# Perceiver block on one core: reductions over the partitions moved from TensorE to VectorE's 32x32 transposes

## The chip, the cores and the metric

The kernel runs on one core of a Trainium2 chip. The metric is device time in microseconds, the median of several runs. The profile is one execution taken by the hardware profiler; its span runs from the first to the last instruction of the core. PE is TensorE's matmuls, PEld its weight loads, DVE is VectorE, ACT is ScalarE, POOL is GpSimd, SP is SyncE.

## What is computed

For each of 16 batches, with x of 128 x 512 and a context of 2048 x 512, all in float32:

```python
x = x + softmax(layernorm(x) @ ctx.T) @ ctx            # cross-attention, one head
x = x + self_attention(layernorm(x))                   # 16 heads of 32, rotary half, causal, then @ Wc
h = layernorm(x)
logits = h[0] @ Wr.T                                   # router: the first token alone, 8 experts
top_vals, top_idx = top_k(logits, 2)                   # gates: softmax over the two
x = x + h + sum(gate[e] * (h @ A[e].T) @ Bw[e].T for e in top_idx)
```

In the last line the expert layer adds its own input h, so that `res` in the kernel starts as x2 + h.

## The kernel before

The work is a software pipeline over the batches. Python generators (`score`, `attend`, `inner`, `experts`) each issue a batch's work in pieces, and the main loop (`for b in range(B - 2)`) steps them by hand so that four batches are under way at once. The order on TensorE is the order of the program, since every matmul, transpose by TensorE and DMA on the SP and ACT queues is kept in program order (`matmul`, `transpose`, `load`). On VectorE, ScalarE and GpSimd a scheduler may move instructions, save those that are `pinned` to the program's order. Helper lines carry most records: line 115 issues for VectorE, ScalarE and GpSimd, line 137 every matmul, 140 every transpose by TensorE, 145 every DMA; so groups are told apart by the tiles' names.

- `score(b)` (from line 376) makes the transposed scores of the cross-attention: the 2048 context rows lie on the partitions (in four blocks of 512, each as four rows per partition), the 128 queries along the free dimension. Matmuls write `psc`, ScalarE copies them to `sc`, VectorE takes the running maximum `mx`. The maximum and the sum of a query's softmax therefore have to be taken over the partitions. For the maximum, `mx` is folded to 128 x 128, TensorE transposes it (`tr_m`), VectorE reduces (`nm`), writes `nm` on a diagonal (`diag`), and a matmul of ones by `diag` (`spread`) brings it to all partitions. VectorE adds `spread` to `sc`, and ScalarE takes the exponentials. `sums` adds up the exponentials of the four blocks, and is folded to `part` (128 x 128).
- `attend(b)` (from line 453) multiplies `sc` with the context in four quarters (`av`); a matmul of `part` by a column of ones gives each query's sum (`den`), its reciprocal is `rden`, and `x1` is `av` times `rden` plus x. The layernorm of x1 follows (`st`, `mv`, `rs`, `h`; `rs`, the root, is GpSimd's).
- `inner(b)` (from line 504) is the self-attention: `v`, `k`, `q` projections, the rotary part (VectorE's shuffle `kP` and product `kT`, GpSimd's product on `kP`, VectorE's add to `kT`; the same for q), head masks `kb` on ScalarE, scores `pss`, softmax in four groups of heads (`att`, `nmx`, `rsm`), transposes of it (`pX`, by way of DRAM to `pT`), `y`, the output product `o`, and `x2`.
- `experts(b)` (from line 889) takes the layernorm of x2 (transposed by way of DRAM to `hT3`). The router multiplies the first token's column with `w_r` (`g_share`) and adds up 4 chunks (`g_part`, 128 x 8); a matmul of ones by `g_part` (`lg`) sums over the partitions and leaves the logits on every partition. `choose` takes the two largest, GpSimd gathers their weights by indirect DMA (`each`, `wb`; `wa` is a copy in another layout), and matmuls `mid` and `ffn` follow; `res` is the result, which a DMA on GpSimd's queue writes out.

In one pass of the main loop TensorE's order is: y of batch b - 1, v of b, tr_m of b + 1, o of b - 1, spread of b + 1, k and q of b, the first quarter of av of b + 1, pss of b, the other quarters of av, den of b + 1, lg of b - 1, psc of b + 2 with mid and ffn of b - 1 inside it. The last batches follow an order written out by hand (`CLOSING`).

A fold and the moves by TensorE, which the change touches:

```python
def halved(t, op):
    vector.tensor_tensor(t[:, :2], t[:, :2], t[:, 2:], op)
    vector.tensor_tensor(t[:, 0], t[:, 0], t[:, 1], op)
    return t[:, 0]
...
transpose(tr[:, :S], most, ident)
vector.tensor_reduce(nm, tr[:, :S], AX.X, ALU.max, negate=True)
vector.tensor_scalar(diag, ident, nm, None, ALU.mult)
matmul(spread[:, :S], ones, diag, start=True, stop=True)
```

Of the kernel before, what the change touches and what calls it, by code (L numbers as in the profile page):

```python
# [11 lines left out]
F32 = mybir.dt.float32  # L12
I32 = mybir.dt.int32
U32 = mybir.dt.uint32
# [75 lines left out]
def perceiver_block(ctx: ExitStack, tc: tile.TileContext, io: dict, out: bass.AP):  # L90
# [40 lines left out]

    padded = const.tile([P, KC, QD], F32, name="padded")
    gpsimd.memset(padded, 0.0)


    def matmul(*args, **kwargs):
# [47 lines left out]
    def norm_pieces(src, name, n=P, tag="h", mix=False):  # L184
        stats = Later(p2, [P, 6], tag="stats", name=f"st_{name}")
        mv = Later(p2, [P, 2], tag="mv", name=f"mv_{name}")
        rstd = Later(p2, [P, 1], tag="rstd", name=f"rs_{name}")
        h = Later(p2 if tag == "h" else p1, [P, D], tag=tag, name=f"{tag}_{name}")

        def root():  # L190
            eps = gpsimd.tensor_scalar_add(rstd[:n], mv[:n, 1:2], EPS)
            if name == "1_1":
                pinned(eps)
            gpsimd.tensor_tensor(rstd[:n], rstd[:n], mhalf[:n], ALU.pow)

        def norm():
            to, of = (mixed(h[:n]), plain(src[:n])) if mix else (h[:n], src[:n])
            return vector.tensor_scalar(to, of, mv[:n, 0:1], rstd[:n], ALU.subtract, ALU.mult)

        return h, [  # L200
            lambda: vector.bn_stats(stats[:n], src[:n]),
            lambda: vector.bn_aggr(mv[:n], stats[:n]),
            root,
            norm,
        ]
# [68 lines left out]
    def named(b, **of):  # L274
        for name, piece in of.items():
            pieces[f"{name}.{b}"] = piece
# [78 lines left out]
    def first_norm(x, hT):  # L355
# [8 lines left out]
        for c in range(KC):  # L364
# [7 lines left out]
            scalar.copy(hT[:, :, c, :], tr[:, :P].rearrange("p (a j) -> p a j", a=4))  # L372
            warm_up(1)


    def score(b):

        hT = p1.tile([P, 4, KC, QD], F32, tag="hT1" if b != 1 else "hT3", name=f"hT1_{b}")
        if b:
            h = layernorm(xs[b], f"1_{b}", mix=b == 1)  # L380
            yield
            transposed(h[:], hT, f"1_{b}", b == 1)
        else:
            first_norm(xs[b], hT)
            yield
        yield

        sc = p2.tile([P, VC, 4, S], F32, tag="sc", name=f"sc_{b}")
        mx = p1.tile([P, 4, S], F32, tag="mx", name=f"mx_{b}")
        for v, ct in enumerate(turned_cts.pop(b)):  # L390
            ps = bank(ps_sc, "sc", f"psc_{b}_{v}").rearrange("p (j t) -> p j t", j=4)
            for j in range(4):

                if v == VC - 1 and j == 3:
                    yield
                for c in range(KC):
                    matmul(
                        ps[:, j, :].rearrange("p (a i) -> p a i", a=4),
                        ct[:, c, j * P : (j + 1) * P], hT[:, :, c, :],
                        start=(c == 0), stop=(c == KC - 1),  # L400
                    )
            scalar.copy(sc[:, v], ps)

            if v:
                vector.tensor_tensor(mx, ps, mx if v > 1 else sc[:, 0], ALU.max)
            if v < VC - 1:
                yield
# [4 lines that stand above are left out]
            return t[:, 0]  # L412

        most = halved(mx, ALU.max)
        yield

        tr = bank(ps_tr, "tr", f"tr_m_{b}")
        transpose(tr[:, :S], most, ident)
        nm = p2.tile([P, 1], F32, tag="nm", name=f"nm_{b}")
        vector.tensor_reduce(nm, tr[:, :S], AX.X, ALU.max, negate=True)  # L420
        diag = p1.tile([P, S], F32, tag="diag", name=f"diag_{b}")
        vector.tensor_scalar(diag, ident, nm, None, ALU.mult)
        yield
        spread = bank(ps_tr, "tr", f"spread_{b}")
        matmul(spread[:, :S], ones, diag, start=True, stop=True)
        for v in range(VC):
            vector.tensor_tensor(
                sc[:, v], sc[:, v], spread[:, None, :S].to_broadcast([P, 4, S]), ALU.add
            )
            scalar.activation(sc[:, v], sc[:, v], AF.Exp)  # L430
        part = p2.tile([P, S], F32, tag="part", name=f"part_{b}")
        scores[b] = (sc, part)
        yield
        sums = p1.tile([P, 4, S], F32, tag="sums", name=f"sums_{b}")
        pinned(vector.tensor_tensor(sums, sc[:, 0], sc[:, 1], ALU.add))
        yield
        for v in range(2, VC):
            pinned(vector.tensor_tensor(sums, sums, sc[:, v], ALU.add))

        def fold():  # L440
            vector.tensor_tensor(sums[:, :2], sums[:, :2], sums[:, 2:], ALU.add)

        def last_fold():
            vector.tensor_tensor(part, sums[:, 0], sums[:, 1], ALU.add)

        if b == B - 1:
            named(b, fold=fold, last_fold=last_fold)
        else:
            fold()
            last_fold()  # L450
        yield

    def attend(b):

        sc, part = scores.pop(b)
        acc = bank(ps_acc, "acc", f"av_{b}")
        ct = cts.pop(b)

        def quarter(v):
            for j in range(4):  # L460
                matmul(
                    acc, sc[:, v, j, :], ct[v][:, j, :],
                    start=(v == 0 and j == 0), stop=(v == VC - 1 and j == 3),
                )

        state = {}

        def whole():
            den = state["den"] = bank(ps_tr, "tr", f"den_{b}")
            matmul(den[:, :1], part, ones[:, :1], start=True, stop=True)  # L470

        rden = Later(p2, [P, 1], tag="rden", name=f"rden_{b}")

        def inverse():
            vector.reciprocal(rden[:], state["den"][:, :1])

        x1 = Later(p2, [P, D], tag="x1", name=f"x1_{b}")

        def added():
            vector.scalar_tensor_tensor(x1[:], acc, rden[:], xs.pop(b), ALU.mult, ALU.add)  # L480

        if b == B - 1:
            quarter(0)
            named(
                b, av1=lambda: quarter(1), av2=lambda: quarter(2), av3=lambda: quarter(3),
                den=whole, rden=inverse, x1=added,
            )
            h, norm = norm_pieces(x1, f"2_{b}", mix=True)
            named(b, **dict(zip(("st2", "mv2", "rs2", "h2"), norm)))
            firsts[b] = x1, h  # L490
            yield
            return
        for v in range(VC):
            quarter(v)
            if v == (VC - 1 if b else VC - 2):
                whole()
                inverse()
            if v < VC - 1:
                yield
        added()  # L500
        firsts[b] = (x1, layernorm(x1, f"2_{b}", mix=b == 0))
        yield

    def inner(b):
# [254 lines left out]
    def shares(b, first):  # L759

        share, part = small(b, E * KC, "share"), small(b, E, "part")
        share = share.rearrange("p (e c) -> p e c", e=E)
        mult = vector.tensor_tensor(
            share,
            w["r"].rearrange("p c e -> p e c"),
            first[:, None, :].to_broadcast([P, E, KC]),
            ALU.mult,
        )
        pinned(mult)
        vector.tensor_reduce(part[:], share, AX.X, ALU.add)  # L770
        return part

    def routing(b):


        z, top, best = small(b, E, "z"), small(b, 8, "top"), small(b, 8, "best", U32)
        at, row, rows = small(b, TOP, "at"), small(b, 1, "row"), small(b, 1, "rows", I32)
        blocks = small(b, TOP, "blocks", I32)

# [7 lines left out]

        def logits(part):

            banks.append(bank(ps_tr, "tr", f"lg_{b}"))  # L790
            matmul(banks[0][:, :E], ones, part[:], start=True, stop=True)

        def choose():
            vector.tensor_copy(z[:], banks[0][:, :E])
            vector.max(top[:], z[:])

            vector.max_index(best[:], top[:], z[:])
            vector.tensor_copy(at[:], best[:, :TOP])
            vector.tensor_scalar(blocks[:], at[:], float(P), column(C_P), ALU.mult, ALU.add)
            vector.tensor_scalar(row[:], at[:, 1:2], column(C_TWOR), column(C_RANK), ALU.mult, ALU.add)  # L800
# [7 lines left out]
                ))  # L808

        def gather_second():  # L810
            gpsimd.indirect_dma_start(
                wb[:], None, io["BT"], bass.IndirectOffsetOnAxis(ap=rows[:], axis=0)
            )

        def joined():

# [72 lines left out]
    def experts(b):  # L889
# [9 lines left out]
        if b < B - 1:  # L899
# [5 lines left out]

            if b < B - 3:
                share()
                yield
                logits(state["part"])
                for piece in rest[:4]:  # L910
                    piece()
                yield
# [137 lines left out]
    for b in range(B - 2):  # L1050
# [17 lines left out]
        step(inner, b)  # L1068
        step(attend, b + 1)
        step(experts, b - 1)  # L1070
        step(inner, b)
        step(experts, b - 1)
        step(inner, b + 1)
# [85 lines left out]
```

## Time and profile before

| what | value |
|---|---|
| time, median of 3 runs | 810.46 us (810.45 to 811.42) |
| the profiled execution's own time | 810.97 us |
| its span | 809.2 us |
| mean granted TensorE clock | 0.998 |
| ACT, POOL busy | 260.4 us, 146.6 us |
| moved by DMA | 211.05 MB, mean 261 GB/s |

In the profile's rows, a start and a duration in us come first, then the engine, the helper's line, the operation, the tile written and those read, shapes and a count; in brackets stands how long the engine had been idle, and what ended it. Equal neighbours are merged into one row. Matmuls overlap: a matmul's duration is its way through the array, so its price in a full queue is the distance from its start to the next one's start. A float32 matmul is two records.

### The profile page before, as it was taken

The page shows a single profiled execution, that of the slowest core. Times are in us where ns is not written, and L with a number is a line of the kernel's source. Part 1 is how long each engine was busy: PE and PEld are TensorE (multiplying, and loading weights), DVE is VectorE, ACT ScalarE, POOL GpSimd, SP SyncE. Part 2 cuts the span into 40 slices and gives each one's busy share as a digit, 9 for nine tenths or more (in the row PEclk, how much of TensorE's full clock was granted, in tenths as well). Part 3 has the DMA queues.
Part 4 walks back from the last instruction along what each step waited for, and adds up shares of the span by engine and source line. Part 5 has one row for each costly group of instructions (what it writes and reads, how often), then busy time and mean ns, then how long its engine had stood idle before and what let it go on. Part 6 is the DMA issues. An engine that isn't in the chain of part 4 may idle for free.

```text
span 809.2 us, 14363 instructions
## 1 busy us (share of the span) xinstructions
PE 800.2 (99%) x5538; PEld 568.5 (70%) x5538; DVE 529.7 (65%) x1234; ACT 260.4 (32%) x772; POOL 146.6 (18%) x213
## 2 busy tenths in 40 slices
PE   9999999999999999999999999999999999999996
PEld 9946775768677576866758677676867757686653
DVE  2455759386684947658495775938667584856885
ACT  2232324142232423233241232415223241422461
POOL 1001011212121121211112121111212112121204
PEclk9999999999999999999999999999999999999999
DMA  9998394967849497694958859495885949664102
GB/s 375 417 389 321 118 380 171 340 253 251 360 163 381 172 324 292 221 397 142 364 212 292 320 188 399 152 353 222 281 337 181 388 152 340 261 231 173 41 1 79
DMA packets 76868, 211.05 MB, mean 261 GB/s; under 512 B 6400, under 2 KB 42624, under 8 KB 60416
## 3 DMA queue, kind: packets, MB, share of 16 engines
q10 hardware_dynamic: 15696, 113.32, 35.0%
q1 hardware_dynamic: 57168, 84.75, 29.4%
q0 software_dynamic: 3936, 12.07, 4.4%
q8 instruction: 44, 0.72, 0.3%
q14 instruction: 24, 0.20, 0.1%
HBM read 180.23 MB, written 29.88 MB: 260 GB/s over the span
## 4 chain that ended last, share of the span: by engine, by line
PE 97%; DVE 1%; POOL 0%; issue 0%; ACT 0%; POOLq 0%
PE psc L137 28%; PE av L137 28%; PE k L137 7%; PE q L137 7%; PE v L137 7%; PE o L137 6%; PE pss_sc L137 2%; PE y L137 2%; PE ffn L137 2%; PE pss_acc L137 2%; PE mid L137 2%; PE warm L137 1%; PE tr_m L140 0%; PE tr L140 0%; PE spread L137 0%; PE lg L137 0%
## 5 line engine op out<-in xcount | busy, mean ns | idle before, releaser
L137 PE MATMUL psc<-hT,ctxT 128*128 128x128 f32 x2048 | 235.0, 276 | 0.0
L137 PEld LDWEIGHTS psc<-hT,ctxT 128*128 128x128 f32 x2048 | 231.3, 192 | 0.5 <-issue 0.5
L137 PE MATMUL av<-ctx,sc 128*128 128x512 f32 x512 | 227.3, 596 | 0.0
L137 PEld LDWEIGHTS av<-ctx,sc 128*128 128x128 f32 x512 | 94.4, 190 | 110.5 <-issue 107.9
L115 ACT ACTIVATE att<-att,nmx 128x128 f32<-128x128 f32 x256 | 98.8, 388 | 84.9 <-DVE nmx L115 84.9
L115 POOL TENSOR_SCALAR rs<-mv 128x1 f32<-128x1 f32 x47 | 10.6, 225 | 431.0 <-DVE g_at L115 209.5
L115 ACT COPY sc<-psc 128x512 f32<-128x512 f32 x64 | 37.5, 586 | 140.0 <-PE psc L137 140.0
L115 ACT ACTIVATE sc<-sc 128x512 f32<-128x512 f32 x64 | 40.2, 630 | 90.9 <-DVE sc L115 90.4
L137 PE MATMUL k<-hT,w_k 128*128 128x128 f32 x512 | 60.1, 275 | 0.0
L137 PE MATMUL q<-hT,w_q 128*128 128x128 f32 x512 | 60.0, 275 | 0.0
L137 PEld LDWEIGHTS k<-hT,w_k 128*128 128x128 f32 x512 | 58.5, 192 | 1.5 <-issue 0.8
L137 PE MATMUL v<-w_v,hT 128*32 128x512 f32 x520 | 59.0, 593 | 0.0
L137 PEld LDWEIGHTS q<-hT,w_q 128*128 128x128 f32 x512 | 58.5, 192 | 0.0
L137 PE MATMUL o<-w_c,yT 128*128 128x512 f32 x128 | 57.8, 594 | 0.0
L115 DVE TENSOR_TENSOR mx<-psc,mx 128x512 f32<-128x512 f32 x32 | 21.6, 676 | 55.0 <-ACT sc L115 55.0
L115 ACT ACTIVATE kb<-kT,cst 128x512 f32<-128x512 f32 (+1 forms) x34 | 36.2, 1113 | 39.8 <-DVE kT L115 39.8
L115 DVE TENSOR_SCALAR h<-x,mv,rs 128x512 f32<-128x512 f32 x47 | 27.4, 583 | 31.9 <-POOL rs L115 31.9
L115 ACT ACTIVATION_READ_ACCUMULATOR att<-att,nmx 128x1 f32 x256 | 47.9, 187 | 0.0
L115 DVE TENSOR_TENSOR sc<-sc,spread 128x512 f32<-128x512 f32 x64 | 42.6, 671 | 3.3 <-PE spread L137 3.3
L115 DVE TENSOR_TENSOR att<-att,rsm 128x512 f32<-128x512 f32 x64 | 43.4, 678 | 0.8
L115 DVE TENSOR_REDUCE nmx<-att 128x4 f32<-128x512 f32 x64 | 41.8, 671 | 0.1
L137 PEld LDWEIGHTS o<-w_c,yT 128*128 128x128 f32 x128 | 23.9, 196 | 23.8 <-issue 23.0
(139 smaller groups left out, 851.1 us busy)
## 6 DMA issues: line engine op xcount, KB each, us to landing
ctx<-in_ctx_dram ACTq DMA_DIRECT2D x56, 1024.0 KB, 8.4
ctxT<-in_ctxT_dram ACTq DMA_DIRECT2D x52, 1024.0 KB, 10.5
there_p<-pX SPq DMA_DIRECT2D x28, 512.0 KB, 4.0
pT<-there_p SPq DMA_DIRECT2D x28, 512.0 KB, 4.5
ctxT<-in_ctxT_dram SPq DMA_DIRECT2D x12, 1024.0 KB, 8.9
there<-blocks SPq DMA_DIRECT2D x42, 256.0 KB, 3.3
hT<-there SPq DMA_DIRECT2D x42, 256.0 KB, 3.0
ctx<-in_ctx_dram SPq DMA_DIRECT2D x8, 1024.0 KB, 10.5
```

What stands on the lines that cost most here:

```text
L115: ins = issue(*args, **kwargs)
L137: tc.keep_in_program_order(nc.tensor.matmul(*args, **kwargs))
```

## The change

For batches from 2 on, the maximum over the partitions no longer goes through TensorE; for batches 2 to 14 the sum doesn't either, and for batches 0 to 12 the router's sum doesn't. A new function does it on VectorE: 32x32 transposes within the tile, a reduction along the free dimension, which leaves one value per quadrant (32 partitions), copies of three quadrants' values to the first quadrant, a second reduction, and then transposes of a broadcast (or four copies of a column) which bring the result to the partitions of all quadrants. More instructions are pinned, the exponentials are issued in two parts, the sums of a batch are pinned behind them and so ahead of the next self-attention's rotary part, `attend` has one step more, and the router's sum follows `share` at once.

```diff
+    beside = const.tile([P, QD], F32, name="beside")
+    gpsimd.memset(beside, 0.0)
...
+    def across(t, name, op, negate=False):
+        n = t.shape[1] // QD
+        turned = p1.tile([P, n, QD], F32, tag="diag" if n == 4 else "turned_1", name=f"turned_{name}")
+        pinned(vector.transpose(turned.rearrange("p q i -> p (q i)"), t))
+        each = p2.tile([P, 4, n], F32, tag=f"each_{n}", name=f"each_quadrant_{name}")
+        pinned(vector.tensor_reduce(each[:, 0, :], turned, AX.X, op))
+        for a in range(1, 4):
+            pinned(vector.tensor_copy(each[:QD, a, :], each[a * QD : (a + 1) * QD, 0, :]))
+        whole = p2.tile([P, n], F32, tag=f"whole_{n}", name=f"whole_{name}")
+        pinned(vector.tensor_reduce(
+            whole[:QD], each[:QD].rearrange("p a q -> p q a"), AX.X, op, negate=negate
+        ))
+        return whole[:QD]
...
+        if b > 1:
+            spread = p1.tile([P, 4, QD], F32, tag="spread", name=f"spread_{b}")
+            peak = across(most, f"m_{b}", ALU.max, negate=True)
+            for a in range(4):
+                pinned(vector.transpose(
+                    spread[a * QD : (a + 1) * QD], peak[:, :, None].to_broadcast([QD, 4, QD])
+                ))
+            for v in range(VC):
+                pinned(vector.tensor_tensor(
+                    sc[:, v], sc[:, v],
+                    spread.rearrange("p j i -> p (j i)")[:, None, :].to_broadcast([P, 4, S]), ALU.add,
+                ))
+                if v < 2:
+                    scalar.activation(sc[:, v], sc[:, v], AF.Exp)
+            yield
+            for v in range(2, VC):
+                pinned(scalar.activation(sc[:, v], sc[:, v], AF.Exp))
...
+            pinned(vector.tensor_tensor(sums, sc[:, 0], sc[:, 1], ALU.add))
+            yield
+            for v in range(2, VC):
+                pinned(vector.tensor_tensor(sums, sums, sc[:, v], ALU.add))
+            yield
+            whole = across(halved(sums, ALU.add), f"den_{b}", ALU.add)
+            vector.reciprocal(whole, whole)
+            rden = p2.tile([P, 1], F32, tag="rden", name=f"rden_{b}")
+            for a in range(4):
+                vector.tensor_copy(rden[a * QD : (a + 1) * QD], whole[:, a : a + 1])
+            scores[b] = (sc, rden)
...
-            if v == (VC - 1 if b else VC - 2):
+            if not known and v == (VC - 1 if b else VC - 2):
                 whole()
                 inverse()
...
-        firsts[b] = (x1, layernorm(x1, f"2_{b}", mix=b == 0))
+        h, norm = norm_pieces(x1, f"2_{b}", mix=b == 0)
+        for piece in norm[:3]:
+            piece()
+        if b:
+            yield
+        pinned(norm[3]())
+        firsts[b] = x1, h
...
+            if b < B - 3:
+                whole = across(part, f"lg_{b}", ALU.add)
+                for a in range(4):
+                    pinned(vector.transpose(
+                        z[a * QD : (a + 1) * QD], whole.to_broadcast([QD, QD])
+                    ))
+                return
...
                 share()
+                logits(state["part"])
                 yield
-                logits(state["part"])
...
         step(experts, b - 1)
+        step(attend, b + 1)
         step(inner, b)
```

On VectorE's queue this puts, in one pass, the whole maximum and the four adds to `sc` and the first add of `sums` ahead of `x2`; the transpose of the third layernorm (`blocks`) and the other two adds of `sums` between `x2` and the shuffle `kP`; the first fold of `sums` (128 x 256) between the product and the add of `kT`, the second (128 x 128) behind that add; the transpose of the sums between the product and the add of `qT`; the rest of the sum between `qT` and the first mask of the self-attention's softmax; and the router's sum between the last groups of that softmax and `x1`. On ScalarE two of the four exponentials stand ahead of the copy `vv` and of the four loads of `ctxT` that follow it. TensorE's order is the same but for the matmuls that are gone.

## Prediction

> **What bounds the kernel now.** I read the page first: the busy row and the chain that ended last.
>
> ```profile
> PE 800.2 (99%) x5538; PEld 568.5 (70%) x5538; DVE 529.7 (65%) x1234; ACT 260.4 (32%) x772; POOL 146.6 (18%) x213
> ...
> PE 97%; DVE 1%; POOL 0%; issue 0%; ACT 0%; POOLq 0%
> ```
>
> PE is in use 99% of the span and carries 97% of the chain. A busy PE need not be at its peak, so next I read one pass of the main loop in the timeline, PE alone.
>
> ```profile
> 393.28 1.08 PE L137 MATMUL y<-pT,vv 128*32 128x128 f32 x32
> ...
> 397.72 0.33 PE L140 MATMUL tr_m<-ident,mx 128*128 128x128 f32 x1
> 397.89 3.60 PE L137 MATMUL o<-w_c,yT 128*128 128x512 f32 x8
> 401.32 0.39 PE L137 MATMUL spread<-diag,ones 128*128 128x128 f32 x2
> 401.55 3.74 PE L137 MATMUL k<-hT,w_k 128*128 128x128 f32 x32
> ...
> 408.69 3.60 PE L137 MATMUL av<-ctx,sc 128*128 128x512 f32 x8
> 412.22 1.13 PE L137 MATMUL pss_sc<-kb,qT 64*128 64x256 f32 x8
> ...
> 424.55 0.28 PE L137 MATMUL den<-ones,part 128*128 128x1 f32 x2
> 424.69 0.37 PE L137 MATMUL lg<-g_part,ones 128*128 128x8 f32 x2
> 424.92 0.91 PE L137 MATMUL psc<-hT,ctxT 128*128 128x128 f32 x6
> ...
> 441.14 1.08 PE L137 MATMUL y<-pT,vv 128*32 128x128 f32 x32
> ```
>
> From y to y is 47.86 us, the same in thirteen passes from 106 us on: PE never waits for data here, so a matmul taken out is worth its own start-to-start time, as long as nothing else comes late. What comes latest shows in VectorE's and GpSimd's timeline ahead of pss, which needs qT.
>
> ```profile
> 401.53 0.69 DVE L115 TENSOR_TENSOR x<-o,x 128x512 f32<-128x512 f32 x1 [2.82 <-PE o L137]
> ...
> 405.10 0.55 DVE L115 TENSOR_SCALAR h<-x,mv,rs 128x512 f32<-128x512 f32 x1 [0.43 <-POOL rs L115]
> ...
> 406.17 0.73 DVE L115 STREAM_SHUFFLE kP<-k 128x512 f32<-128x512 f32 x1
> 406.98 1.28 POOL L115 TENSOR_TENSOR kP<-kP,cst 128x512 f32<-128x512 f32 x1 [1.91 <-DVE kP L115]
> 408.29 0.69 DVE L115 TENSOR_TENSOR kT<-kT,kP 128x512 f32<-128x512 f32 x1 [0.20 <-POOL kP L115]
> 409.12 0.74 DVE L115 STREAM_SHUFFLE qP<-q 128x512 f32<-128x512 f32 x1
> 411.31 0.69 DVE L115 TENSOR_TENSOR qT<-qT,qP 128x512 f32<-128x512 f32 x1 [0.89 <-POOL qP L115]
> ```
>
> qT is ready at 411.31 + 0.69 = 412.00 and pss starts at 412.22. In the tail, where PE does wait, tr follows the end of h by 0.05 us (800.03 to 800.08). So only 0.22 - 0.05 = 0.17 us of cover is left at pss. That is the place of this prediction.
>
> **What the change takes off PE.** Start to start, unrounded: tr_m 0.166, spread 0.221, den 0.140, lg 0.223, together 0.750 us a pass. Passes 1 to 13 lose all four; the score of b = 15 loses the first two (0.39). If PE never waited: 13 x 0.750 + 0.39 = 10.1 us. The built order on PE is otherwise unchanged.
>
> **What it adds to VectorE.** Each reduction is a 32x32 transpose, a reduce, three copies between quadrants, a reduce, and four more moves or transposes. Rows near: 128-wide operations take 0.29 us, tiny ones 0.14 to 0.18. Maximum: 0.29 + 0.29 + 3 x 0.14 + 0.17 + 4 x 0.29 = 2.3, less nm and diag (0.58): +1.7. Sum: 0.29 + 0.29 + 0.42 + 0.17 + 0.16 + 4 x 0.14 = 1.9, less rden: +1.75. Router: about 1.6, less the copy g_z: +1.5. So some 5 us a pass beside 32.5 us of VectorE work in 47.86: VectorE doesn't become the bound. What counts is where they stand.
>
> *Maximum, up to x2.* From the start of y: the last mx at -0.14 (441.00 against 441.14); with 0.73, 0.46 and 0.33 the transpose is at 1.37, the reduce at 1.71, res at 1.92 (ends 2.60), copies from 2.63. No row shows a move between quadrants. The Trainium skill (VectorE: DVE Perf Modes, Two Vector instructions with no wait between them) says that an instruction whose start quadrant changes is held until all earlier ones have finished. Unheld, small rows follow each other by 0.05 to 0.1 us and 128-wide ones by 0.21 (g_nm to mv 0.05, mx to res 0.21); held, by their length and 0.035: 0.175 and 0.33. Unheld the three copies and four transposes take about 1.1 us, held 1.9. I take held: second reduce 3.16, transposes from 3.36, the four adds of sc from 4.70 at 0.605 each, sums at 7.11, VectorE free at 7.72. x2 can start at 401.53 - 393.28 = 8.25, less tr_m's 0.17: 8.08. Cover 0.36 us held, about 1.1 unheld; either way x2 isn't late. Below nothing it can't go, since x2 waits for o.
>
> *From x2 to qT.* x2 follows o, but k now starts right behind o: against PE's program x2 comes 0.22 later. Before, sc's adds filled the waits of the layernorm chain x2, st, mv, rs, h. Now they are done before, and what used to stand behind qT (two adds of sums) and the transpose of h stand between h and kP. By rows: x2 to st 0.73, st to mv 0.73, mv to h 1.18, h to blocks 0.58, blocks to the next 0.64, sums to sums 0.80, to kP 0.60: 5.26 us, where it was 406.17 - 401.53 = 4.64. That is +0.62.
>
> Between the kT multiply and kT's add now stands the fold of sums (128x256, two inputs in SBUF), while GpSimd multiplies kP. No row has just this pair; the nearest is in the tail:
>
> ```profile
> 793.90 0.95 POOL L115 DMA_INDIRECT wb<-in_BT_dram,g_rows  x1 [0.30 <-issue]
> ...
> 794.45 1.08 DVE L115 TENSOR_TENSOR res<-x,h 128x512 f32<-128x512 f32 x1
> ...
> 751.27 0.68 DVE L115 TENSOR_TENSOR res<-x,h 128x512 f32<-128x512 f32 x1
> ```
>
> The same add takes 0.68 alone and 1.08 beside GpSimd: it ends 0.68 after GpSimd's end (794.85 to 795.53), so it waited it out. The skill (SBUF — State Buffer, Who interferes with whom) says the same of a VectorE instruction with two SBUF inputs beside a GpSimd one that reads SBUF: the later is blocked whole. POOL's kP starts 0.08 after the shuffle and takes 1.28; the fold comes 0.4 into it, is blocked to its end, takes 0.42, and kT's add follows 0.34 after POOL's end where it was 0.03: +0.31. Without the block the fold is free. I take the block (row and rule agree), and keep 0 as the other bound. The second fold and den's transpose stand in waits that last longer.
>
> qT is then late by 0.22 + 0.62 + 0.31 - 0.17 = 0.98 us, and PE waits that long ahead of pss, with av, psc and all else in its queue behind. kb is at hand 0.5 us ahead of that (0.78 ahead of pss before).
>
> *Hidden.* The rest of the sum stands between qT and the first mask, which it holds to about y + 21.0 (before: 414.90 - 393.28 = 21.62). The router's steps put x1 some 1.2 us later; behind it h2's way through SP's queue ends 4.8 us ahead of v (hT issued 434.20, 3.0 to land, v 442.03) and wa 3.2 us ahead of mid (435.17, 438.40): covered. On ACT two exps now stand ahead of vv, so vv's copy and the four ctxT loads behind it come 2.2 to 2.7 us later; q needs vv's bank 4 us after that, ctxT is used at y + 31.6 and lands by about y + 20. The pinned GpSimd gathers keep their place; the memset is once.
>
> **Sum.** A pass: -0.750 + 0.98 = +0.23. Thirteen: +3.0. The score of b = 15: no adds of sums and no fold ahead of kP, its shuffle at x2 + 3.9, no wait: -0.39. Together +2.6. The profiled execution took 810.97 with a span of 809.2; it is 0.5 above the median, so 813.6 for it is 810.46 + 2.6 = 813.1 for the median.
>
> **Rivals.**
> - *Likeliest, 42%*: as above, 813.1 (812.0 to 814.5 for 0.1 us either way at pss).
> - *No block, 17%*: the fold runs beside POOL's kP. Wait 0.67, a pass -0.08, together -1.5: 808.9. For it: the row that shows a block has an indirect DMA on POOL, not a multiply.
> - *Copies blocked too, 25%*: POOL issues out's DMA (0.67 us) 0.3 after res, at y + 2.9 to 3.56, just where the third copy between quadrants stands. If it waits that out, the adds of sc end 0.58 later, x2 is 0.22 late, a pass +0.45: about 816. Against it: no row shows such a DMA blocking a tiny copy.
> - *Faster, 8%*: the wait at pss doesn't arise, since kP's shuffle comes within 4.64 - 0.22 + 0.17 = 4.6 us of x2. From there PE keeps all it is given: 810.46 - 10.1 = 800.3. For it: DVE has 15 us free a pass. Against: seven rows make the 5.26, and the instructions' order is fixed. Each 0.1 us between is worth 1.3 us.
> - *Slower still, 8%*: moves between quadrants or transposes of 32 partitions cost over 0.1 us more than the nearest rows, beyond the 0.36 of cover, or the waits lower PE's clock (0.5 in the tail behind waits of 2.6 and 0.7 us): over 817.5. Against the clock: the tail's first wait of 0.7 us left it at 1.
>
> The range leaves out the last two: 808.6 to 817.5. A measurement of this kernel can tell 0.2% (1.6 us) from no change. Faster by that: the 8%, and 6 of the 17: 0.14. Within: the other 11, and 8 from the likeliest's low edge: 0.19. Slower: 0.67.
>
> **What would show it.** In the profile after: tr_m, spread, den, lg gone from the passes; y to y 48.1; a PE idle of about 1 us ahead of each pss, put down to qT; sums of 128x256 about 1.2 us long; x2 still led by PE o. Without PE idle there, or with the fold at 0.42, the steps above are wrong; idle DVE ahead of x2 gone means the copies.

## The result, and the profile after

The changed kernel takes 813.05 us (median of 9 runs, 812.05 to 816.36), the kernel before beside it on the same chip 810.94 us (9 runs). The ratio is 1.0029, 95% interval 1.0017 to 1.0042: slower by 2.1 us, and above the 0.2% that can be told from no change. The prediction was 813.1. The profiled execution took 812.06 us, with a span of 810.3.

The page's busy row and the chain that ended last, of the changed kernel:

```profile
PE 790.0 (98%) x5444; PEld 559.8 (69%) x5444; DVE 612.2 (76%) x1593; ACT 258.2 (32%) x772; POOL 146.4 (18%) x214
...
PE 79%; DVE 13%; POOL 4%; issue 3%; DMA 0%; POOLq 0%; ACT 0%; DVEq 0%
```

PE has lost 10.2 us of work (800.2 before), as computed, and the span is longer all the same. The chain says why: it now leaves PE for VectorE and GpSimd 17% of the time. One pass of PE's timeline, the seventh, shows where:

```profile
394.61 1.08 PE L139 MATMUL y<-pT,vv 128*32 128x128 f32 x32
...
399.05 3.70 PE L139 MATMUL o<-w_c,yT 128*128 128x512 f32 x8
402.59 3.73 PE L139 MATMUL k<-hT,w_k 128*128 128x128 f32 x32
...
414.16 1.13 PE L139 MATMUL pss_sc<-kb,qT 64*128 64x256 f32 x8 [0.82 <-DVE qT L115]
...
442.62 0.65 PE L139 MATMUL y<-pT,vv 128*32 128x128 f32 x16
```

tr_m, spread, den and lg are gone. From the start of one y to the start of the next, which is called a pass below, it is 48.01 us where it was 47.86. In brackets stands the wait that took their place: pss waits for qT, and the list of PE's waits (total, how often, longest) has it in all thirteen passes and next to nothing else in the loop:

```profile
PE pss_sc L139 <- DVE qT L115: 11.1, 13, 1.3
```

VectorE and GpSimd ahead of that wait, the same pass:

```profile
402.79 0.69 DVE L115 TENSOR_TENSOR x<-o,x 128x512 f32<-128x512 f32 x1 [0.42 <-PE o L139]
...
406.65 1.45 DVE L115 TENSOR_TENSOR sums<-sums,sc 128x512 f32<-128x512 f32 x2
408.02 0.73 DVE L115 STREAM_SHUFFLE kP<-k 128x512 f32<-128x512 f32 x1
...
408.83 1.28 POOL L115 TENSOR_TENSOR kP<-kP,cst 128x512 f32<-128x512 f32 x1 [3.43 <-DVE kP L115]
409.24 1.15 DVE L115 TENSOR_TENSOR sums<-sums 128x256 f32<-128x256 f32 x1
410.31 0.68 DVE L115 TENSOR_TENSOR kT<-kT,kP 128x512 f32<-128x512 f32 x1
...
413.32 0.69 DVE L115 TENSOR_TENSOR qT<-qT,qP 128x512 f32<-128x512 f32 x1 [0.67 <-POOL qP L115]
```

x2 is still led by PE's o, so the maximum is in time. From x2 on VectorE has no gap up to kT's add but that of the layernorm: the two adds of sums and the fold fill it, and qT ends at 414.01.

All passes take 48.00 to 48.03 us, but for the first (48.47, where the first add of sums stood between h and its transpose) and the ninth (48.17, where ffn and the y behind it came later). Thirteen passes are 2.66 us longer than before, the fourteenth, of b = 15, is 0.29 shorter: +2.37. The two profiled spans differ by only 1.1, since in the execution profiled before the granted clock was 0.5 for 3.4 us in the tail, worth about 1.2 us (from the last y to the end it is 17.9 us there and 16.7 here), and in this one it stayed at 1.00 behind a wait just as long (2.5 us for wa). The medians differ by 2.1.

### The profile page after: what moved, and what is told of

Its sections match the earlier page's. It is cut to its first block, busy times and chain, and to the rows that moved or that the text cites. A ratio compares the mean times of both kernels' runs of the same rounds, so it can differ in the third digit from the quotient of the medians.

```text
span 810.3 us, 14522 instructions
## 1 busy us (share of the span) xinstructions
PE 790.0 (98%) x5444; PEld 559.8 (69%) x5444; DVE 612.2 (76%) x1593; ACT 258.2 (32%) x772; POOL 146.4 (18%) x214
## 4 chain that ended last, share of the span: by engine, by line
PE 79%; DVE 13%; POOL 4%; issue 3%; DMA 0%; POOLq 0%; ACT 0%; DVEq 0%
PE psc L139 28%; PE av L139 22%; PE v L139 7%; PE o L139 7%; DVE sums L115 2%; PE pss_sc L139 2%; POOL qP L115 2%; DVE kT L115 2%; PE y L139 2%; PE pss_acc L139 2%; PE ffn L139 2%; PE mid L139 2%; POOL rs L115 1%; PE k L139 1%; PE q L139 1%
## 5 line engine op out<-in xcount | busy, mean ns | idle before, releaser
L115 ACT ACTIVATE sc<-sc 128x512 f32<-128x512 f32 x64 | 38.2, 627 | 69.9 <-DVE sc L115 56.0
L115 DVE TENSOR_TENSOR sc<-sc,spread 128x512 f32<-128x512 f32 x64 | 40.0, 686 | 3.8 <-PE spread L139 3.3
```

The costliest lines, as they stand in the source:

```text
L115: ins = issue(*args, **kwargs)
```

## The experiments

Theory (order): PE pays for what stands on VectorE between x2 and qT, nothing else of the change costs. Rivals: VectorE is fuller and late everywhere (load); or the fold that GpSimd blocks is the cost (lock). All kernels are the changed kernel with the edits that are named, but for the ninth, which is the kernel before with one edit.

**1. Sums behind qT** (`e1_sums_behind_qT`): the two wide adds of sums, and all behind them, follow qT's add.

```diff
             pinned(vector.tensor_tensor(sums, sc[:, 0], sc[:, 1], ALU.add))
             yield
+            yield
             for v in range(2, VC):
                 pinned(vector.tensor_tensor(sums, sums, sc[:, v], ALU.add))
-            yield
```

> The last two adds of sums move from between x2 and kP to behind the add of qT, where they stood before the change; all else as changed. Order theory (the PE wait at pss is made by what stands between x2 and qT): kP comes about 1.4 us earlier, more than the 0.89 us that PE waits at pss, so the wait is gone, a pass is 48.02 - 0.89 = about 47.13 us, the time about 813 - 12 = 801. Load theory (VectorE is 76% in use instead of 65%, and PE waits because of that): the load is the same, so the time stays at 813. Lock theory (the fold that GpSimd blocks is what costs): the fold leaves kP's product here too, so 801 as well; the next run tells those two apart.

Measured: 839.97 us (832.35 to 856.59, 4 runs). The wait at pss is gone, undisturbed passes take 47.12 us as computed, and the kernel is still slower by far: other passes take up to 57.94. PE's waits name another place.

```profile
PE v L139 <- DMA hT<-there: 20.9, 4, 9.1
```

So the mechanism at pss is right, load is refuted (the same work fits), and a second limit stands right behind it: hT2, the second layernorm, which is written to DRAM and fetched from there transposed, lands late. The timeline's DMA issues and v around one such pass:

```profile
195.97 0.82 ACTq L147 DMA_DIRECT2D ctx<-in_ctx_dram  x2
196.16 0.37 SPq L147 DMA_DIRECT2D hT<-there  x1
211.30 5.05 PE L139 MATMUL v<-w_v,hT 128*32 128x512 f32 x32 [9.09 <-DMA hT<-there]
```

and the same issues in the changed kernel:

```profile
435.19 0.37 SPq L147 DMA_DIRECT2D hT<-there  x1
437.46 2.00 ACTq L147 DMA_DIRECT2D ctx<-in_ctx_dram  x4
443.52 1.04 PE L139 MATMUL v<-w_v,hT 128*32 128x512 f32 x8
```

with, from the page's list of issues for that stretch, KB and us to landing:

```profile
hT<-there SPq DMA_DIRECT2D x1, 256.0 KB, 4.1
```

Issued 2.3 us ahead of the four ctx loads (4 MB on ScalarE's queue), hT2 lands in 4.1 us. Issued 0.2 us behind them it ends v's wait only 15.1 us after its issue. The lead of the fetch over the first of these loads, pass by pass: before 1.8 to 3.8 us, changed kernel 1.3 to 2.7, here 0.9 and less. x1 explains most of it: it stands 15.6 us ahead of the next y before, 14.4 in the changed kernel, 12.5 to 13.9 here. The rest differs from pass to pass, since the fetch also waits until its own write to DRAM (`there<-blocks`) has landed, 2.1 to 3.6 us in the changed kernel. The lead alone does not decide: the waits of 5 us and more came at leads of -0.2, 0.1 and 0.8 us, while ten other passes with leads of 0.5 to 0.9 waited 0.4 us or not at all. What makes that difference is open.

**2. One reduction for the two folds** (`e2_fold_by_reduce`): one instruction with one input takes the place of the fold that was held up.

```diff
-            whole = across(halved(sums, ALU.add), f"den_{b}", ALU.add)
+            folded = p2.tile([P, S], F32, tag="part", name=f"folded_sums_{b}")
+            vector.tensor_reduce(folded, sums.rearrange("p a s -> p s a"), AX.X, ALU.add)
+            whole = across(folded, f"den_{b}", ALU.add)
```

> The two folds of sums (two inputs in SBUF) become one tensor_reduce over the four (one input in SBUF, about as long as 0.67 us, which ends within GpSimd's product on kP). Order theory: kT's add follows GpSimd's end by 0.03 instead of 0.20 us, so a pass gains 0.17 us and the time is about 813 - 2.2 = 810.8; the PE wait at pss falls from 0.89 to about 0.72. Lock theory: the whole wait goes, 801. If the fold was only slow by itself, the time stays at 813.

Measured: 812.13 us (811.13 to 813.15, 12 runs), ratio to before 1.0017 (1.0009 to 1.0026). Passes 47.91 to 47.94 but for the first, 0.09 less, about half of what was expected. The reduction took 1.07 us, not 0.67, and lets kT's add start 0.08 after GpSimd's end, where the fold did 0.20. Lock as the main cause falls.

**3. The router alone on VectorE** (`e3_router_alone`): maximum and sum by TensorE again (`if b > 1` made `if False`, `known = False`, the last batch's folds named as before).

> Only the router's sum goes over VectorE; maximum and sum of the softmax are TensorE's again, in their order of before. Order theory: nothing new stands between x2 and qT, so PE keeps what lg cost it (0.22, and 0.09 in the next psc, which followed lg more slowly): 13 x 0.31 = 4.0 us below the kernel before, about 806.9. Load theory: 1.5 us more VectorE a pass, of the change's 6.1, so a PE wait of a quarter of 0.89: 13 x (0.22 - 0.31), about 810.

Measured: 813.92 us (808.01 to 819.55, 20 runs), ratio 1.0034 (1.0012 to 1.0056). Passes take 47.63 us, 0.22 less than before: lg's price, not the 0.31 that was expected (experiment 7 says why). And yet runs spread over 11 us. The profiled one (810.35) has v waiting for hT2 once, for 1.0 us; its fetches lead the loads by 0.7 to 1.9 us. The expectation missed this.

**4. One add more** (`e4_one_add_more`): the first add of sums done a second time between x2 and kP.

> The first add of sums is done a second time, between x2 and kP (it writes the same values again). Order theory: it stands between h and blocks and puts off all behind it by about 0.48 us, and every bit of that is PE's: 13 x 0.48 = +6.2, about 819. Load theory: VectorE has 9 us free in a pass, 0.6 more hardly shows: 813 to 815.

Measured: 820.76 us (820.41 to 821.65, 4 runs), ratio 1.0121 (1.0105 to 1.0138). Passes 48.48, +0.46. The order is what PE pays for. The first pass lost 2.4 more, so the total is above the expectation: there PE waited 2.07 us for qT, and the granted clock (the number ahead of the last two) was about 0.5 for the next 3.4 us. The waits of 1.28 us in the other passes left it at 1.00.

```profile
126.94 1.24 PE L139 MATMUL pss_sc<-kb,qT 64*128 64x256 f32 x8 [2.07 <-DVE qT L115]
```

```profile
127.80:131.20 3.40, 3.40 (x14) 2.13 (x11) 3.23 (x9) 1.08 (x6) 0.00 (x0) 0.51 0.43 148
```

**5 to 8. Order, folds, and the loads' place.** Experiment 5 is the first one with the four loads of ctx issued later:

```diff
-        load_ctx(b + 2)
         step(score, b + 2)
         step(experts, b - 1)
+        load_ctx(b + 2)
         step(score, b + 2)
```

> The order with the sums' last two adds behind qT's add, and besides the four loads of ctx (4 MB, ScalarE's queue) issued some 4 us later, behind the copy of mid in place of the copy of the third psc. Theory: what spoilt that order before was only that the four loads were issued 0.5 us or less behind the fetch of hT2 (in the changed kernel 2.4 us, in the kernel before 3.3 us), so that hT2's 256 KB shared the 16 DMA engines with 4 MB and v waited for it. With 4 us more between them, every pass should take 47.12 us, v should wait nowhere, and the median should be 801 us, with a narrow interval. Rival, hT2 is late because x1 is late on VectorE whatever the loads do: v still waits 5 to 9 us in some passes, and the median stays at 820 to 840 us.

Measured: 804.59 us (803.97 to 807.02, 6 runs), ratio to before 0.9926 (0.9914 to 0.9939). v waits nowhere; this version beats both kernels by more than 6 us. Passes are 47.12 at the least; the thirteen together take 4.1 us more than thirteen times that, the longest 48.74:

```profile
530.97 1.16 PE L139 MATMUL mid<-hT,wa 128*128 128x128 f32 x8 [1.15 <-POOL wa L115]
```

mid waits for the chosen experts' weights: the choice stands behind x1 on VectorE, and its gathers come late. Nearly all of the 4.1 us is lost just ahead of mid, the rest at pss.

Experiment 6 is the changed kernel with the same loads one step earlier (ahead of the `step(score, b + 2)` that precedes them).

> The changed kernel with nothing altered but the place of the four loads of ctx on ScalarE's queue: ahead of the copy of the third psc, so some 3.5 us earlier, about 1 us ahead of the fetch of hT2 instead of 2.4 us behind it. Theory of the loads: hT2 then lands some 14 us after its issue in every pass, v waits 5 to 9 us in each of 13 passes, and the time is 870 to 930 us. Rival, the loads don't matter for hT2: no change, 812 us.

Measured: 939.31 us (935.69 to 941.09, 5 runs), ratio 1.1596 (1.1579 to 1.1613). Nothing was touched on VectorE or PE, and v waits up to 7.6 us in twelve passes, 84 us together. The time is 126 us longer than the changed kernel's, so the waits are not all. Stretches of 3.4 us at one of them show where much of the rest is (after the busy times: granted clock, DMA share, GB/s):

```profile
155.31 1.08 PE L139 MATMUL y<-pT,vv 128*32 128x128 f32 x32
163.89 6.57 PE L139 MATMUL v<-w_v,hT 128*32 128x512 f32 x32 [7.50 <-DMA hT<-there]
```

```profile
159.60:163.00 3.40, 0.00 (x0) 0.00 (x0) 3.10 (x6) 1.23 (x2) 0.00 (x0) 0.50 0.74 291
163.00:166.40 3.40, 2.51 (x12) 0.67 (x16) 0.00 (x0) 0.00 (x0) 0.00 (x0) 0.50 0.02 6
166.40:169.80 3.40, 3.40 (x20) 0.90 (x16) 0.00 (x0) 0.00 (x0) 0.00 (x0) 0.50 0.00 0
169.80:173.20 3.40, 3.40 (x15) 1.37 (x8) 0.00 (x0) 1.06 (x2) 0.00 (x0) 0.99 0.45 116
```

The clock falls to 0.5 some 3 us into the wait, stays there for another 6 us behind its end at 163.89, and v takes 6.57 instead of 3.62.

Experiment 7 is experiment 3 with the loads late.

> Maximum and sum of the softmax by TensorE as before, the router's values by VectorE, and the four loads of ctx some 4 us later. Theory of the loads: the waits of v for hT2 that spread the runs of the same kernel with loads in their old place (808 to 819.5 us) are gone, passes of 47.63 us, 806.9 us with a narrow interval. Rival, the router's steps delay x1 and so hT2 in themselves: still 808 to 819 us, spread.

Measured: 808.20 us (807.69 to 809.32, 6 runs), ratio 0.9970 (0.9959 to 0.9982). Twelve passes at 47.63 or 47.64, no wait for hT2, and the spread is 1.6 us instead of 11.5, so the spread of experiment 3 came from the loads. The time is 1.3 above the expectation, which had counted 0.09 a pass for psc besides lg's 0.22. That doesn't come: psc's first matmul takes 0.19 us to the next one's start behind den here as behind lg before, and 0.11 behind av in the changed kernel. 13 x 0.09 is 1.2 us.

Experiment 8 holds the folds behind qT's add and leaves the loads.

```diff
-            vector.tensor_tensor(t[:, :2], t[:, :2], t[:, 2:], op)
+            first = vector.tensor_tensor(t[:, :2], t[:, :2], t[:, 2:], op)
+            if op is ALU.add:
+                pinned(first)
```

> The changed kernel, the two folds of the sums and the first transpose (turned_den) held behind qT's add; the two 512-wide adds of the sums stay where they are, and the loads too. Theory of the order: the first fold cost 0.17 us (kT's add starts 0.20 us after GpSimd's end instead of 0.03), the second 0.21 us between kT's add and qP; together 0.38 us of the wait of 0.82 us at pss go, passes take 47.64 us, and the time is about 807 us. Rival, only the two wide adds matter (1.37 us) and the folds are hidden by GpSimd's products: no change, 812 us.

Measured: 828.51 us (827.88 to 830.27, 5 runs), ratio 1.0220 (1.0207 to 1.0234). Two misses. The passes take 47.86, 0.15 less, not 0.38: from kT's add to qP is 0.81 us with or without the second fold, so that one was free. And x1 came 1.1 us later against the next y than in the changed kernel; in two passes the fetch led the loads by only 0.16 and 0.03 us, v waited 11.8 us in all, and those passes, with the clock, cost 17.0 us.

**9. The kernel before with the loads late** (`e9_before_loads_late`).

> The kernel before, with only the four loads of ctx moved 3.5 us later on ScalarE's queue, as in the version that beat both kernels (804.6 us). Theory: in the kernel before hT2's fetch is issued 1.8 to 3.8 us ahead of these loads and v waits for nothing, so there is nothing to gain: passes of 47.86 us, 810.8 us, within 0.2%. Rival: the later place is worth several microseconds by itself, and the gain of that version is none of the change's: about 804 us.

Measured: 811.27 us (810.28 to 812.16, 13 runs), ratio 1.0004 (0.9995 to 1.0012), passes 47.86. So the gain of experiment 5 isn't that of the loads: they only allow it.

**10. Maximum and sum alone** (`e10_softmax_alone_loads_late`): experiment 5 with the router's sum back on TensorE (both tests `b < B - 3` in `shares` and `logits` made `False`).

> The version that beat both kernels, with the router's sum over the partitions back on TensorE (matmul with ones); maximum and sum of the softmax stay on VectorE, the sums' adds behind qT, the loads late. TensorE gets back 0.22 us a pass (what the router alone had given): 47.34 us. VectorE loses the router's transposes and copies of 1.7 us ahead of the choice and of x1. Theory: the version's passes over 47.12 us (13 passes took 4.0 us more than 13 times that) come from the choice of the experts, late on VectorE, by way of the gathers and the matmul mid; with 1.7 us less ahead of it they go, and the time is 804.6 + 13 x 0.22 - 4.0 = 803.5 us. Rival, those waits are of the DMA engines and not of VectorE's order: they stay, 807.5 us.

Measured: 926.60 us (926.01 to 928.25, 5 runs), ratio 1.1433 (1.1417 to 1.1448). A plain miss: I had costed what lg takes from PE and not where it stands.

```profile
422.12 0.59 PE L139 MATMUL lg<-g_part,ones 128*128 128x8 f32 x2 [6.99 <-DVE g_part L115]
```

lg stands in PE's queue ahead of the last two quarters of av, and in this order VectorE gives g_part some 7 us too late for it. There are 13 such waits, 86.7 us together, and the granted clock is 0.94 over a pass. The place is the changed program's: its router's sum follows `share` at once, a step ahead of where the kernel before had lg, behind all of av and den. In that old place lg would hardly have waited, by an estimate: the two quarters of av take 6.9 us, and PE reached lg 7.0 us too early. That wasn't run, so it is not shown that this order needs the router off PE, nor was the question about the choice answered.

**11. The choice first** (`e11_choice_first`): experiment 5 with the choice of the experts and the two gathers of A ahead of x1, by one more step.

> The version that beat both kernels, with the choice of the experts and its two gathers of A ahead of x1 on VectorE and GpSimd (they stood behind it). Gathers 1.6 us earlier, x1 0.9 us later, layernorm 2 some 1.5 to 2.5 us later. Theory as above: the waits of mid for wa go and passes are 47.12 us: 800.6 us. Rival, hT2's fetch, now issued some 3.5 us ahead of y in place of 6, lands too late for v: waits there take the gain, 803 to 815 us.

Measured: runs of 801.84, 801.97, 804.34, 814.47 and 815.99 us. The ratio of the three lowest to before is 0.9904 (0.9886 to 0.9922). In the profiled run (801.97) ten of the thirteen passes take 47.12 or 47.13, and mid no longer waits in them: the theory of the choice holds. But the fetch of hT2 now comes only 3 us ahead of y, and three passes wait for it some tenths of a us. Of the two high runs there is no trace; a caught fetch would fit them, and that isn't shown.

**12. The loads on hT2's own queue** (`e12_loads_behind_hT2`): experiment 11 with the four loads on SyncE's queue, right behind the fetch.

```diff
         fetch(f"2_{b + 1}")
+        queue = nc.sync
+        load_ctx(b + 2)
+        queue = nc.scalar
```

> The version with the choice of the experts ahead of x1, with one thing altered: the four loads of ctx go out on SyncE's queue, directly behind the fetch of hT2, in place of ScalarE's queue 1.2 to 2 us behind it. Theory: hT2 was held up only by loads of another queue that shared the 16 DMA engines with it; on its own queue they stand behind it, however late it is. Then v waits at most some tenths of a us (for the fetch issued 3 us ahead of y), passes take 47.12 us, and all runs lie at 800.5 to 802.5 us, none at 814. Rival, loads of the same queue share the DMA engines with hT2 just the same: they now come 0.5 us behind it, as in the version that spoilt the order of the sums (0.5 us and less), so v waits 5 to 9 us in several passes, 820 us or more.

Measured: 806.52 us (801.23 to 809.86, 10 runs), ratio 0.9938 (0.9917 to 0.9958). On the question asked, the theory holds: loads issued 0.5 us behind hT2, on its own queue, make v wait at most 0.75 us. The time doesn't follow: in the profiled run (807.85) one pass took 52.17.

```profile
537.86 0.96 ACTq L147 DMA_DIRECT2D ctxT<-in_ctxT_dram  x2
549.78 0.33 ACTq L147 DMA_DIRECT2D ctxT<-in_ctxT_dram  x1
550.17 1.15 ACT L115 ACTIVATE sc<-sc 128x512 f32<-128x512 f32 x2 [11.76 <-DMA ctx<-in_ctx_dram]
```

The second and third ctxT loads of this pass take 0.96 us to issue; the fourth goes out only 11 us later. In the trace it waits for the semaphore that the fourth ctx load raises when it has landed, and ScalarE's exponentials and kb stand behind it, so kb came 2.9 us late for pss. The granted clock was 0.5 for 3.4 us after that wait. The same wait is there in eleven of the thirteen passes: in most of them the fourth ctxT load goes out 12 to 15 us behind the start of y, here 18.3, and in experiment 11, with all these loads on ScalarE's queue, 7 to 8. So the move to the other queue brought the wait. Why it ended some 3 us later in this pass is open. Experiment 5 is the fastest version whose runs stay close together.

## Why the prediction was right

*TensorE's share, -0.750 a pass.* All four are gone. Two neighbours changed: o's first matmul takes 0.53 us to the next one's start instead of 0.43, now that it stands behind v and not behind tr_m (+0.10), and psc's first takes 0.11 behind av instead of 0.19 behind lg (-0.08). Net -0.73.

*The maximum is in time.* Right, by the held price. The moves:

```profile
397.25 0.50 DVE L115 COPY each_quadrant_m<-each_quadrant_m 32x4 f32<-32x4 f32 x3
...
397.51 0.67 POOL L115 DMA_DIRECT2D out_dram<-res  x1 [6.72 <-DVE res L115]
...
397.99 1.25 DVE L115 STREAM_TRANSPOSE spread<-whole_m 32x128 f32<-32x128 f32 x4
```

Copies follow each other by 0.17 us and transposes by 0.31, where I took 0.175 and 0.33, so nothing overlaps. sums starts at y + 7.07 (7.11). GpSimd's DMA issue does begin in the middle of the three copies, and they take 0.50 together all the same: the rival "copies blocked too" falls. x2 starts at y + 8.18, 0.10 later than predicted, by o.

*From x2 to kP, 5.26.* Measured 5.23.

*The block, +0.31.* Right in kind, mis-sized: 0.17. The fold took 1.15 and ended 0.28 after GpSimd's end, not 0.42, and kT's add started 0.20 after it, not 0.34. The Trainium skill (SBUF — State Buffer, Who interferes with whom) has the later instruction blocked whole; here the fold did about a third of its work beside GpSimd or faster than alone. Experiments 2 and 8 put the block's worth at 0.09 and 0.15 a pass, so neither the whole block nor the rival without one fits.

*The cover, 0.17.* Mis-sized the other way: pss follows the end of qT's add by 0.146, not by the 0.05 that I took from the tail, so only 0.07 of the 0.22 was cover. Together PE waits 0.887 a pass where 0.98 was predicted, and a pass is -0.73 + 0.89 = +0.155 instead of +0.23.

*VectorE's work.* It grew by about 6 us a pass (82.5 us in all), where I had 5. That moved nothing, since it is the places that count.

*Hidden.* x1 came 1.23 us later against the next y (1.2), the first mask at y + 21.22 (21.0), v waits nowhere: right for this kernel. But the cover of hT2 was measured by the wrong thing. I took 4.8 us from its landing to v, at its undisturbed 3.0 us (in that pass of the kernel before it took 3.8). What counts is the lead of its issue over the four ctx loads, and there the change used up about 1 us of some 3. With x1 another 0.8 us closer to y (experiment 3), v waited 1.0 us in one pass; with 1.1 (experiment 8), 5.2 and 6.6 us in two; with up to 1.9 (experiment 1), 5 to 9 us in three. The prediction's faster rival named the right place and price (800.3 if nothing waits at pss), and said nothing of this limit; experiment 5 came within 4.3 us of it, and the low runs of experiments 11 and 12 within 1.6, all with the loads moved.

*Last batch, -0.39.* Measured -0.29, the same 0.10 at o. First and ninth passes, +0.46 and +0.15, were not foreseen. Sum +2.4 against +2.6: near, with errors that partly cancel. That the totals agree within 0.1 us (813.1 and 813.05) is luck: the prediction started from a median of 810.46, and the kernel before took 810.94 beside the changed one, where the medians differ by 2.1.

## What to carry to other kernels

When the engine that bounds a kernel gives work to a neighbour, count what the neighbour then does between the bound's last product and its next demand, instruction by instruction; the neighbour's mean load (65% to 76% here) said nothing about it. Measure the cover of a transfer by the lead of its issue over the next large burst from another queue as well as by its landing. And when an order is freed at one place, look for the next demand that becomes late: here qT, then hT2, then wa.

## What the runs showed of the hardware

- A transfer of 256 KB that lands in 4.1 us when issued 2.3 us ahead of a 4 MB burst from another queue takes 15 us when issued 0.2 us behind it. With the burst on its own queue, 0.5 us behind it, v waited 0.75 us at most. With leads of 0.5 to 0.9 us, both happened. In experiment 1, from 195.9 to 212.5 us, ScalarE's queue moved 4.19 MB in 576 packets (7.3 KB each), SyncE's 1.03 MB in 1178 (0.9 KB). The Trainium skill (DMA: Bandwidth & Descriptors, Queues, rings and completion order) says that a DMA engine takes turns between queues packet by packet; then each small packet of hT2 waits for a large one of ctx, which would fit the 15 us. No run here changed the packets' size.
- In a wait of 7.5 us TensorE's granted clock fell to 0.5 and stayed there for 6 us behind the wait's end; v took 6.57 us instead of 3.62 (experiment 6). Behind a single wait of 2.07 us it was about 0.5 for 3.4 us (experiment 4). Waits of 0.8 us (the changed kernel) and 1.28 us (experiment 4) at pss left it at 1.00, and so did one of 2.5 us in the changed kernel's tail, which in the kernel before was followed by 3.4 us at 0.5.
- A reduction over the partitions on VectorE, here the maximum of a 128x128 tile with its spreading back, takes 3.3 us from the transpose to the last move (395.99 to 399.24), with one other instruction of 0.68 between.
- A DMA's issue on a compute engine's queue that has to wait for a landing holds that engine's work behind it: in experiment 12 ScalarE stood idle for 11.76 us behind an issue that itself took 0.33 us. Four issues that needn't wait take 2.00 us (changed kernel, at 437.46).
